# The last 40 steps of an LSTM in a graph layer: one PSUM bank for gate G of each half, another order of products, and moved copies

## The chip, the core and the metric

The kernel runs on one core of a Trainium2 chip. Its engines work side by side, each through its own queue in order: TensorE (PE, with a row PEld for its weight loads), VectorE (DVE), ScalarE (ACT), GpSimd (POOL), and SyncE (SP), which issues DMAs here. The metric is the device time of one execution in microseconds (us); lower is better.

## What is computed

The layer takes 6,250 nodes of 256 features and 100,000 edges. It normalizes the rows, adds a sum over neighbours with a small MLP and a linear attention block, normalizes again, and runs an LSTM over the 6,250 rows as one sequence:

```
def step(carry, xp):                      # xp = x W_ih^T + b_ih + b_hh
    h, c = carry
    gates = xp + h @ W_hh.T
    i, f, g, o = jnp.split(gates, 4, axis=-1)
    c = jax.nn.sigmoid(f) * c + jax.nn.sigmoid(i) * jnp.tanh(g)
    h = jax.nn.sigmoid(o) * jnp.tanh(c)
```

On each output h a two-way argmax of a linear map decides whether h counts; prefix and suffix sums of the counted ones, weighted, are added to 2h and to the input of the LSTM.

## The kernel before

The sequence of 6,250 rows is cut into `NC` = 125 chains of `NS` = 50 rows each, which go through the LSTM together: one step of the kernel handles row s of all chains. Since a chain needs the state that its predecessor ends with, each chain is warmed up by running `WARM` = 40 rows of the predecessor first; a comparison at the end tests whether warmed and true states agree, and a sequential fallback follows if they don't. So there are 90 steps. The first 50 (40 of warm-up, and rows 0 to 9 of the counted pass) compute the inputs' product x W_ih on the way and are not touched here. The warm-up stores that product with the bias to DRAM (`x_d`), and the last 40 steps, rows `KEPT` = 10 to 49, fetch it again (`fetch`, L989, three tiles `x_in` in turn) and add only the product of h with `w_hh`.

In these last 40 steps everything lies with units on the partitions: 256 units are `KD` = 2 halves (a = 0, 1) of 128, and h's 256 units are also the contraction, in two parts (k = 0, 1). A gate g of a half a takes one product for each k, a 128x128 weight block against 128x125 of h; a float32 product shows as two PE records. A step so has 16 products. Gates are I, F, G, O; I, F and O of one half share a PSUM bank, in slots 0 to 2, so that one sigmoid of 375 columns serves the three. G has a bank of its own in which both halves lie, for one tanh of 250 columns. There are two sets of these three banks, one for even and one for odd steps (`sets`, L1083). Two further banks (`pl`) are for the logits.

Before the products of a step can accumulate, its fetched inputs must be in the banks. `into_banks` (L1086) returns three moves: G of both halves, I/F/O of half 0, I/F/O of half 1. In the first two of the 40 steps they are matmuls by an identity with start=True, later they are copies on ACT.

The order on PE, DVE and ACT is as written (a manual schedule). For step s:

- PE (L1109 to L1114): products with k = 0 of G of both halves and of I, F, O of half 0; the same with k = 1; then I, F, O of half 1 with k = 0 and with k = 1; then the two products of the logits of step s - 1. k = 0 reads half 0 of h of the step before, k = 1 reads half 1.
- ACT: tanh of G (L1116); for each half the sigmoid (L1119), one of the moves for step s + 1 (L1121), and the tanh of c (L1127); then the third move (L1132).
- DVE: for each half, `two` (I times tanh G beside F times c, L1124), the add that gives c (L1125), a correction of h of step s - 2 (`weighted`, L882), and h itself (L1130); then `summed` (L884), which thresholds the logits and sums.
- SP: the fetch of step s + 4's inputs at the end of the step, into the tile whose moves the step has just made.

The tile `gc` holds, for each half, tanh of G and c side by side, so that one DVE instruction multiplies both.

Of the kernel before, what the change touches and what calls it, by code (L numbers as in the profile page):

```python
# [14 lines left out]
F32 = mybir.dt.float32  # L15
I32 = mybir.dt.int32
BF16 = mybir.dt.bfloat16
AF = mybir.ActivationFunctionType
# [5 lines left out]
P = 128  # L24
# [3 lines left out]
NC, NS = 125, 50  # L28
HEADS, HC = 8, 32
KD = D // P  # L30
# [51 lines left out]
def gps_layer(ctx: ExitStack, tc: tile.TileContext, x, src, dst, cols, rows, kvln, wqkv, mw1, mw2, gw1, gw2,  # L82
              wih, whh, blstm, out):
    nc = tc.nc
# [7 lines left out]
    ident = big.tile([P, P], F32, name="ident")  # L92
# [66 lines left out]
    with ExitStack() as s1:  # L159
# [54 lines left out]
        with tc.tile_pool(name="ln1", bufs=2) as lp, tc.tile_pool(name="ps0", bufs=6, space=PSUM) as ps:  # L214
# [3 lines left out]
            for i, t in enumerate((src, dst)):  # L218
                s = behind[:, i * (FULL + 1) * P:(i + 1) * (FULL + 1) * P].bitcast(I32).rearrange("p (b e) -> p b e", e=P)
# [35 lines left out]
            for s, to in zip(tiled, (si, drel)):  # L255
                f = late[:, 2 * GE:2 * GE + (FULL + 1) * P].rearrange("p (b e) -> p b e", e=P)
# [126 lines left out]
        ps = s1.enter_context(tc.tile_pool(name="ps1", bufs=4, space=PSUM))  # L383
# [13 lines left out]
        to = [sums[:, k, :N].rearrange("p (c s) -> p s c", s=NS) for k in range(KD)]  # L397
# [5 lines left out]
        def gather(at):  # L403
            g = edge_p.tile([P, D], F32, name="eg", bufs=10)
            nc.gpsimd.indirect_dma_start(out=g, out_offset=None, in_=xn_d[:],  # L405
                                         in_offset=bass.IndirectOffsetOnAxis(ap=at, axis=0))
            return g
# [41 lines left out]
        def kv_job(j):  # L449
# [4 lines left out]
            def product(k, half):  # L454
                at = slice(half * D, (half + 1) * D)
                nc.tensor.matmul(pkv[:r, at], xnT[:, j, k, :], w_qkv[:, k, D:][:, at],  # L456
                                 start=(k == 0 and half == 0), stop=(k == KD - 1), skip_group_check=True)

            yield [partial(product, k, half) for k in range(KD) for half in range(2)], None
            flat = mix_p.tile([P, 2 * D], F32, name="kv", tag="t", bufs=4)  # L460
            nc.vector.tensor_add(flat[:r], pkv[:r], kv_bias[:r])  # L461
# [214 lines left out]
        def bias_job():  # L676

            b_r = [mix_p.tile([P, 2 * D], F32, name="b_r", tag="t", bufs=4) for _ in range(2)]
            for i in range(2):
                nc.sync.dma_start(b_r[i][:2], blstm[:, i * 2 * D:(i + 1) * 2 * D])  # L680
            yield [], None
            yield [], None
            pb = ps.tile([P, BANK], F32, name="mm")

            def product(g):
                at = g * P % (2 * D)
                nc.tensor.matmul(pb[:, g:g + 1], b_r[g * P // (2 * D)][:2, at:at + P], ones[0:2, 0:1], start=(g == 0),
                                 stop=True, skip_group_check=True)

            yield [partial(product, g) for g in range(4 * KD)], None  # L690
            nc.vector.tensor_copy(b_l, pb[:, :4 * KD])
# [41 lines left out]
        with tc.manual_schedule(engines={mybir.EngineType.PE, mybir.EngineType.DVE, mybir.EngineType.Activation}):  # L733
# [3 lines left out]
            while slot < GROUPS - COUNTED or running or before or any(s >= slot for s in starts):  # L737
                g = slot + COUNTED
# [24 lines left out]
        w_hh = big.tile([P, KD, 4 * D], F32, name="w_hh", tag="M2")  # L763
# [5 lines left out]
        with tc.If(held < GROUPS + PAIRS):  # L769
# [15 lines left out]
            with tc.For_i(0, NE, 1) as c:  # L785
# [4 lines left out]
                g = gather(at[:, :1])  # L790
                for n0 in range(0, N + W, W):
# [4 lines left out]
                    for k in range(KD):  # L796
                        nc.tensor.matmul(pm[:, k, :w], g[:, k * P:(k + 1) * P], here[:, 0, :w], start=(k == 0), stop=True,
                                         skip_group_check=True)
# [24 lines left out]
        for a in range(KD):  # L823
            nc.vector.tensor_scalar(scaled[:, a, :], ident, sc[:, a:a + 1], None, op0=ALU.mult)
            nc.tensor.matmul(pb[:, a * P:(a + 1) * P], mean[:, a:a + 1].to_broadcast([P, P]), ident, start=(a == 0),
                             stop=True, skip_group_check=True)
# [12 lines left out]
    I, F, G, O = range(4)  # L839

    SLOT = {I: 0, F: 1, O: 2, G: 3}

    def block(g, a):
        return slice((g * KD + a) * P, (g * KD + a + 1) * P)
# [9 lines left out]
    gc = wl.tile([P, KD, 2, NC], F32, name="gc")  # L854
# [17 lines left out]
    def of_step(s):  # L872
        return hs[:, :, s * NC:(s + 1) * NC]

    def logits(s, pl):
        for k in range(KD):
            nc.tensor.matmul(pl, w_d[:, k, :], of_step(s)[:, k, :], start=(k == 0), stop=(k == KD - 1))

    def weighted(s, i, of, k):

        h_k = of_step(s)[:, k, :]
        nc.vector.scalar_tensor_tensor(h_k, of[:, k, :], half[:, i, k:k + 1], h_k, op0=ALU.mult, op1=ALU.add)  # L882

    def summed(s, pool, pl):  # L884

        w = pool.tile([P, KD, NC], F32, name="w")
        nc.vector.scalar_tensor_tensor(w, pl[:, None, :].to_broadcast([P, KD, NC]), thr, of_step(s), op0=ALU.is_gt,
                                       op1=ALU.mult)
        if s == 0:
            nc.vector.tensor_copy(inc, w)  # L890
        else:
            nc.vector.tensor_add(inc, inc, w)
        for k in range(KD):
            weighted(s, 2, inc, k)
        return w
# [20 lines left out]
    with tc.tile_pool(name="lstm", bufs=2) as rp:  # L916
        AHEAD, FETCH = 3, 3
        s2 = ExitStack()
        ps = s2.enter_context(tc.tile_pool(name="ps3", bufs=4, space=PSUM))
# [69 lines left out]
        def fetch(s):  # L989
            t = rp.tile([P, KD, 4, NC], F32, name="x_in", bufs=FETCH)  # L990
            nc.sync.dma_start(t.rearrange("p k g c -> p (k g c)"), x_d[(s - NS + WARM) * P:(s - NS + WARM + 1) * P, :])
            return t
# [30 lines left out]
        KEPT = NS - WARM  # L1023
# [25 lines left out]
        fetched = []  # L1049
        for i, (s, warm) in enumerate(order):  # L1050
# [18 lines left out]
            if not warm and s > 0:  # L1069
# [7 lines left out]

        s2 = ExitStack()  # L1080
        ps = s2.enter_context(tc.tile_pool(name="ps_k", bufs=1, space=PSUM))
        ps_y = s2.enter_context(tc.tile_pool(name="ps_l", bufs=2, space=PSUM))
        sets = [([ps.tile([P, 3, NC], F32, name=f"pg{i}{a}") for a in range(KD)], ps.tile([P, KD, NC], F32, name=f"pg_g{i}"))  # L1083
                for i in range(2)]

        def into_banks(s, t):  # L1086


            others_a, g_b = sets[s % 2]
            parts = [(g_b, t[:, :, SLOT[G], :])] + [(others_a[a], t[:, a, :SLOT[G], :]) for a in range(KD)]  # L1090
            if s < KEPT + 2:
                return [partial(nc.tensor.matmul, to, ident, of, start=True, stop=False, skip_group_check=True)
                        for to, of in parts]
            return [partial(nc.scalar.copy, to, of) for to, of in parts]

        def product(s, g, a, k):
            others_a, g_b = sets[s % 2]
            to = g_b[:, a, :] if g == G else others_a[a][:, SLOT[g], :]
            nc.tensor.matmul(to, w_hh[:, k, block(g, a)], of_step(s - 1)[:, k, :], start=False, stop=(k == KD - 1),  # L1099
                             skip_group_check=True)  # L1100

        with tc.manual_schedule(engines={mybir.EngineType.PE, mybir.EngineType.DVE, mybir.EngineType.Activation}):
            for bring in into_banks(KEPT, fetched.pop(0)):
                bring()
            fetched.append(fetch(KEPT + FETCH))
            w = None
            for s in range(KEPT, NS):
                more = into_banks(s + 1, fetched.pop(0)) if s + 1 < NS else []
                for k, a_ifo in ((0, 0), (1, 0), (0, 1), (1, 1)):  # L1109
                    gates = [(I, a_ifo), (F, a_ifo), (O, a_ifo)]  # L1110
                    for g, a in gates if a_ifo else [(G, a) for a in range(KD)] + gates:
                        product(s, g, a, k)
                pl = ps_y.tile([P, BANK], F32, name="pl")[:, :NC]
                logits(s - 1, pl)  # L1114
                others_a, g_b = sets[s % 2]
                nc.scalar.activation(gc[:, :, 0, :], g_b, AF.Tanh)  # L1116
                for a in range(KD):
                    gates = rp.tile([P, 4, NC], F32, name="gates")[:, :SLOT[G], :]
                    nc.scalar.activation(gates, others_a[a], AF.Sigmoid)  # L1119
                    for bring in more[a:a + 1]:  # L1120
                        bring()  # L1121

                    two = rp.tile([P, 2, NC], F32, name="two", tag="h_w")
                    nc.vector.tensor_mul(two, gates[:, :2, :], gc[:, a])  # L1124
                    nc.vector.tensor_add(c[:, a, :], two[:, 0, :], two[:, 1, :])  # L1125
                    t_c = rp.tile([P, NC], F32, name="t_c")
                    nc.scalar.activation(t_c, c[:, a, :], AF.Tanh)  # L1127
                    if w is not None:
                        weighted(s - 2, 0, w, a)
                    nc.vector.tensor_mul(of_step(s)[:, a, :], gates[:, SLOT[O], :], t_c)  # L1130
                for bring in more[KD:]:
                    bring()  # L1132
                w = summed(s - 1, rp, pl)
                if s + 1 + FETCH < NS:
                    fetched.append(fetch(s + 1 + FETCH))
            for k in range(KD):
                weighted(NS - 2, 0, w, k)
# [4 lines left out]
        parts = rp.tile([P, 2], F32, name="parts", bufs=1)  # L1142
# [16 lines left out]
    with tc.If(right < 2 * D * (NC - 1)):  # L1159
        one_by_one = ExitStack()  # L1160
        rp = one_by_one.enter_context(tc.tile_pool(name="lstm1", bufs=2))
        ps = one_by_one.enter_context(tc.tile_pool(name="ps3b", bufs=2, space=PSUM))
# [9 lines left out]
        with tc.For_i(0, NC, 1) as c0:  # L1172
# [3 lines left out]
            pg = ps.tile([P, NG, NS], F32, name="pg1")  # L1176
            for g in range(NG):
                at = slice(g * P, (g + 1) * P)
                nc.tensor.matmul(pg[:, g, :], ident, bl_r[:, g, :], start=(g == 0), stop=False, skip_group_check=True)
                for k in range(KD):  # L1180
                    nc.tensor.matmul(pg[:, g, :], w_ih[:, k, at], yb[:, k, :], start=False, stop=False,
                                     skip_group_check=True)
            for t in range(NS):
                for g in range(NG):
                    for k in range(KD):
                        last = h0[:, k:k + 1] if t == 0 else hb[:, k, t - 1:t]
                        nc.tensor.matmul(pg[:, g, t:t + 1], w_hh[:, k, g * P:(g + 1) * P], last, start=False,
                                         stop=(k == KD - 1), skip_group_check=True)
# [96 lines left out]
```

## Time and profile before

| What | us |
|---|---|
| median of 3 runs | 1590.43 (1588.79 to 1592.89) |
| the profiled execution, its own time | 1589.72 |
| span of its profile | 1587.9 |
| last 40 steps, first product to last h | 1337 to 1536 |

The profile is of one execution, and its times add up against its own time. A line of the timeline has the start in us from the span's beginning, the duration, the engine, the line of the kernel, the operation, what it writes and reads, and how many instructions of the same kind were merged; in square brackets stand the idle time in front of it and what ended it. PE records overlap, since matmuls are pipelined and their ends are modelled. A line of waits has who waited for whom, the total in us, how many times, and the longest. A table by stages has the window, its length, and for each engine the busy time with the number of instructions; then the clock granted to TensorE (1.00 is full speed), the share of time in which the DMA engines were busy, and GB/s.

### The profile page before, as it was taken

Reading aid. Unit: us, or ns where it says so; the run is one execution under the profiler, and the core shown is the slowest. Engines: PE = TensorE matmul, PEld = TensorE weight load, DVE = VectorE, ACT = ScalarE, POOL = GpSimd, SP = SyncE. Lnnn points to the kernel's source line nnn. Section 1 sums busy time; section 2 is a strip of 40 time slices with the busy share of each in tenths; the row PEclk is TensorE's granted clock in tenths of the full one; section 3 lists DMA queues with packets and bytes.
Section 4 is the critical chain, followed back from the end, with each engine's and each line's share of the span. In section 5 each row is a group of like instructions: output and inputs, shape, how many; then the busy total and the mean of one; then the engine's idle time right before and its main releaser. Section 6 shows DMA issues by size and latency. Waiting matters only on the chain. (4 is left out here: it accounts for less than half of the span.)

```text
span 1587.9 us, 30599 instructions
## 1 busy us (share of the span) xinstructions
PE 1442.4 (91%) x11164; PEld 1366.3 (86%) x11164; DVE 968.8 (61%) x3002; ACT 600.6 (38%) x1742; POOL 682.0 (43%) x715
## 2 busy tenths in 40 slices
PE   1789999999989999999999689999999999999965
PEld 1488888888989999999989689999999999888864
DVE  6789888888842222222222366666676655777777
ACT  2843334333402222233233234444444433555530
POOL 2177777777777777777777300000000000000005
PEclk9689999999999999999999989999999999999986
DMA  9533333333354555444444321111111100333315
GB/s 249 191 104 103 104 103 104 105 105 105 105 159 137 152 153 149 124 116 123 121 122 117 111 91 53 66 66 53 65 66 63 44 1 27 105 105 105 104 38 163
DMA packets 64644, 165.97 MB, mean 105 GB/s; under 512 B 14350, under 2 KB 29440, under 8 KB 63232
## 3 DMA queue, kind: packets, MB, share of 16 engines
q0 software_dynamic: 31008, 84.71, 18.5%
q1 hardware_dynamic: 29822, 75.08, 14.5%
q10 hardware_dynamic: 3652, 4.10, 1.1%
q8 instruction: 91, 1.49, 0.4%
q14 instruction: 71, 0.58, 0.1%
HBM read 130.56 MB, written 33.28 MB: 103 GB/s over the span
## 5 line engine op out<-in xcount | busy, mean ns | idle before, releaser
L405 POOL DMA_INDIRECT eg<-xn_d,si x646 | 621.4, 962 | 260.6 <-issue 99.3
L426 PE MATMUL pg<-here,eg 128*128 128x96 f32 x2584 | 389.4, 276 | 30.3 <-DMA eg<-xn_d,si 28.1
L426 PEld LDWEIGHTS pg<-here,eg 128*128 128x128 f32 x2584 | 355.7, 194 | 61.0 <-DMA eg<-xn_d,si 29.2
L436 DVE TENSOR_TENSOR sums<-sums,pg 128x192 f32 x162 | 57.4, 354 | 343.9 <-PE pg L426 183.9
L976 PE MATMUL pg<-yT,w_ih 128*128 128x125 f32 x1600 | 189.5, 277 | 0.5 <-ACT yT L967 0.5
L976 PEld LDWEIGHTS pg<-yT,w_ih 128*128 128x128 f32 x1600 | 185.3, 194 | 0.8 <-ACT yT L967 0.8
L942 POOL TENSOR_TENSOR ln_r<-ln_v,minus_half 125x1 f32<-125x1 f32 x50 | 27.3, 550 | 322.9 <-DVE ln_v L936 322.9
L1009 ACT ACTIVATE gates<-pg,b_l 128x125 f32<-128x125 f32 x398 | 111.9, 364 | 132.3 <-PE pg L1000 79.6
L1214 POOL TENSOR_TENSOR xr<-xr,rest_t 125x1024 f32<-125x1024 f32 x8 | 22.9, 2895 | 287.2 <-DVEq L1159 287.2
L1000 PE MATMUL pg<-h_w,w_hh 128*128 128x125 f32 x1248 | 145.9, 275 | 0.1
L1000 PEld LDWEIGHTS pg<-h_w,w_hh 128*128 128x128 f32 x1248 | 143.1, 192 | 0.3 <-DVE x_out L985 0.3
L628 ACT ACTIVATE sums<-mm,vec 128x125 f32<-128x125 f32 x100 | 36.5, 366 | 239.0 <-DVE sums L436 176.4
L1099 PE MATMUL pg<-sums,w_hh 128*128 128x125 f32 x960 | 120.3, 275 | 0.0
L612 PE MATMUL mm<-sums,g 128*128 128x125 f32 x800 | 116.3, 280 | 1.9 <-DVE counts L651 1.1
L1099 PEld LDWEIGHTS pg<-sums,w_hh 128*128 128x128 f32 x960 | 113.6, 192 | 0.0
L623 PE MATMUL mm<-z,g 128*128 128x125 f32 x800 | 112.6, 279 | 0.5 <-ACT z L618 0.5
L612 PEld LDWEIGHTS mm<-sums,g 128*128 128x128 f32 x800 | 103.4, 193 | 5.8 <-issue 1.6
L456 PE MATMUL mm<-m,xr 128*125 128x256 f32 x400 | 107.6, 397 | 0.3 <-DVE counts L651 0.3
L623 PEld LDWEIGHTS mm<-z,g 128*128 128x128 f32 x800 | 99.8, 192 | 0.7 <-ACT z L618 0.7
L464 ACT ACTIVATE mm<-kv 125x512 f32<-125x512 f32 x50 | 30.1, 602 | 183.3 <-DVE kv L461 183.3
L618 ACT ACTIVATE z<-mm,vec 128x125 f32<-128x125 f32 x200 | 56.4, 367 | 94.8 <-PE mm L612 94.8
L416 DVE TENSOR_TENSOR here<-counts,drel 128x384 f32<-128x384 f32 x162 | 90.1, 556 | 0.0
(273 smaller groups left out, 2340.5 us busy)
## 6 DMA issues: line engine op xcount, KB each, us to landing
x_d<-x_out SPq DMA_DIRECT2D x40, 500.0 KB
x_in<-x_d SPq DMA_DIRECT2D x40, 500.0 KB
eg<-xn_d,si POOLq DMA_INDIRECT x646, 2.8
counts<-xn_d SPq DMA_DIRECT2D x16, 384.0 KB
xn<-in_x_dram SPq DMA_DIRECT2D x5, 1120.0 KB
xn_d<-xn SPq DMA_DIRECT2D x5, 1120.0 KB
m<-in_x_dram SPq DMA_DIRECT2D x50, 112.0 KB
out_dram<-o SPq DMA_DIRECT2D x12, 448.0 KB
```

What stands on the lines that cost most here:

```text
L405: nc.gpsimd.indirect_dma_start(out=g, out_offset=None, in_=xn_d[:], in_offset=bass.IndirectOffsetOnAxis(ap=at, axis=0))
L416: nc.vector.tensor_tensor(here[:, :n, :], iota[:, None, :W].to_broadcast([P, n, W]), drel[:, gi * GT:gi * GT + n, None].to_broadcast([P, n ...
L426: nc.tensor.matmul(pg[:, k, :], g[:, k * P:(k + 1) * P], here[:, i, :], start=(i == 0 and k == 0), stop=(i == n - 1), skip_group_check=True)
L436: nc.vector.tensor_add(window, window, pg)
L456: nc.tensor.matmul(pkv[:r, at], xnT[:, j, k, :], w_qkv[:, k, D:][:, at], start=(k == 0 and half == 0), stop=(k == KD - 1), skip_group_chec ...
L612: nc.tensor.matmul(p1[:, m, :], g1[:, k, m * P:(m + 1) * P], sums[:, k, at], start=(m == 0 and k == 0), stop=(k == KD - 1), skip_group_che ...
L618: nc.scalar.activation(z1[:, m, :], p1[:, m, :], AF.Relu, bias=col("gb1", m))
L623: nc.tensor.matmul(p2[:, a, :], g2[:, m, a * P:(a + 1) * P], z1[:, m, :], start=(a == 0 and m == 0), stop=(m == 2 * KD - 1), skip_group_ch ...
L976: nc.tensor.matmul(pg[:, SLOT[g], :], w_ih[:, k, block(g, a)], yT[:, k, s * NC:(s + 1) * NC], start=(i == 0 and k == 0), stop=False, skip_ ...
L1000: nc.tensor.matmul(banks[a][:, SLOT[g], :], w_hh[:, k, block(g, a)], h[:, k, :], start=False, stop=(k == KD - 1), skip_group_check=True)
L1009: nc.scalar.activation(gate[g], pg[:, SLOT[g], :], AF.Tanh if g == G else AF.Sigmoid, bias=bias(g, a))
L1099: nc.tensor.matmul(to, w_hh[:, k, block(g, a)], of_step(s - 1)[:, k, :], start=False, stop=(k == KD - 1), skip_group_check=True)
```

## The change

Four things change in the last 40 steps; the products, activations and DVE work on them stay the same in kind and in amount of data.

- The banks: G of each half has a bank of its own, used by every step (two banks, `bank_g`); I/F/O keep two banks for each half (`bank_o`). It is six banks in all, as before.
- The products: the k = 0 group has G, I, F, O of half 0 and I of half 1; the k = 1 group has G, I, F, O of half 0; then come G of half 1 with both k, F and O of half 1 with k = 0, and I, F, O of half 1 with k = 1.
- The tanh of G is made for each half apart: half 0 before the sigmoid of half 0, half 1 behind it.
- The moves of inputs, now four a step: I/F/O of half 0 of the next step at the head of a step, G of half 0 after the second tanh of G, G of half 1 and I/F/O of half 1 behind the sigmoid of half 1, ahead of the tanh of c of half 1. I/F/O are moved by PE in the first two steps, G in the first step only.

```diff
-        sets = [([ps.tile([P, 3, NC], F32, name=f"pg{i}{a}") for a in range(KD)], ps.tile([P, KD, NC], F32, name=f"pg_g{i}"))
-                for i in range(2)]
...
+        bank_g = [ps.tile([P, NC], F32, name=f"pg_g{a}") for a in range(KD)]
+        bank_o = [[ps.tile([P, SLOT[G], NC], F32, name=f"pg{i}{a}") for a in range(KD)] for i in range(2)]
+
+        def bring(s, t, gate_g, a):
+
+            to, of = (bank_g[a], t[:, a, SLOT[G], :]) if gate_g else (bank_o[s % 2][a], t[:, a, :SLOT[G], :])
+            if s < KEPT + (1 if gate_g else 2):
+                nc.tensor.matmul(to, ident, of, start=True, stop=False, skip_group_check=True)
+            else:
+                nc.scalar.copy(to, of)
+
+        def products(s, *of):
+            for g, a, k in of:
+                to = bank_g[a] if g == G else bank_o[s % 2][a][:, SLOT[g], :]
+                nc.tensor.matmul(to, w_hh[:, k, block(g, a)], of_step(s - 1)[:, k, :], start=False, stop=(k == KD - 1),
+                                 skip_group_check=True)
...
             for s in range(KEPT, NS):
-                more = into_banks(s + 1, fetched.pop(0)) if s + 1 < NS else []
-                for k, a_ifo in ((0, 0), (1, 0), (0, 1), (1, 1)):
-                    gates = [(I, a_ifo), (F, a_ifo), (O, a_ifo)]
-                    for g, a in gates if a_ifo else [(G, a) for a in range(KD)] + gates:
-                        product(s, g, a, k)
+                more = s + 1 < NS
+                t = fetched.pop(0) if more else None
+                if more:
+                    bring(s + 1, t, False, 0)
+                products(s, (G, 0, 0), (I, 0, 0), (F, 0, 0), (O, 0, 0), (I, 1, 0))
+                products(s, (G, 0, 1), (I, 0, 1), (F, 0, 1), (O, 0, 1))
+                products(s, (G, 1, 0), (G, 1, 1), (F, 1, 0), (O, 1, 0), (I, 1, 1), (F, 1, 1), (O, 1, 1))
                 pl = ps_y.tile([P, BANK], F32, name="pl")[:, :NC]
                 logits(s - 1, pl)
-                others_a, g_b = sets[s % 2]
-                nc.scalar.activation(gc[:, :, 0, :], g_b, AF.Tanh)
                 for a in range(KD):
+                    if a == 0:
+                        nc.scalar.activation(gc[:, 0, 0, :], bank_g[0], AF.Tanh)
                     gates = rp.tile([P, 4, NC], F32, name="gates")[:, :SLOT[G], :]
-                    nc.scalar.activation(gates, others_a[a], AF.Sigmoid)
-                    for bring in more[a:a + 1]:
-                        bring()
+                    nc.scalar.activation(gates, bank_o[s % 2][a], AF.Sigmoid)
+                    if a == 0:
+                        nc.scalar.activation(gc[:, 1, 0, :], bank_g[1], AF.Tanh)
+                    if more:
+                        bring(s + 1, t, True, a)
+                    if a and more:
+                        bring(s + 1, t, False, 1)
...
-                for bring in more[KD:]:
-                    bring()
                 w = summed(s - 1, rp, pl)
```

More of the change, by code (lines that the diff above doesn't have):

```diff
@@ L1082, in gps_layer @@
         ps_y = s2.enter_context(tc.tile_pool(name="ps_l", bufs=2, space=PSUM))
-        sets = [([ps.tile([P, 3, NC], F32, name=f"pg{i}{a}") for a in range(KD)], ps.tile([P, KD, NC], F32, name=f"pg_g{i}"))
-                for i in range(2)]
-        def into_banks(s, t):
-            others_a, g_b = sets[s % 2]
[L1090 to L1100, printed above, removed]
+        bank_g = [ps.tile([P, NC], F32, name=f"pg_g{a}") for a in range(KD)]
[11 more added lines that the diff above has]
+                                 skip_group_check=True)
         with tc.manual_schedule(engines={mybir.EngineType.PE, mybir.EngineType.DVE, mybir.EngineType.Activation}):
-            for bring in into_banks(KEPT, fetched.pop(0)):
-                bring()
+            t = fetched.pop(0)
+            for gate_g in (False, True):
+                for a in range(KD):
+                    bring(KEPT, t, gate_g, a)
             fetched.append(fetch(KEPT + FETCH))
@@ L1107, in gps_layer @@
             for s in range(KEPT, NS):
-                more = into_banks(s + 1, fetched.pop(0)) if s + 1 < NS else []
-                for k, a_ifo in ((0, 0), (1, 0), (0, 1), (1, 1)):
-                    gates = [(I, a_ifo), (F, a_ifo), (O, a_ifo)]
-                    for g, a in gates if a_ifo else [(G, a) for a in range(KD)] + gates:
-                        product(s, g, a, k)
+                more = s + 1 < NS
[5 more added lines that the diff above has]
+                products(s, (G, 1, 0), (G, 1, 1), (F, 1, 0), (O, 1, 0), (I, 1, 1), (F, 1, 1), (O, 1, 1))
                 pl = ps_y.tile([P, BANK], F32, name="pl")[:, :NC]
                 logits(s - 1, pl)
-                others_a, g_b = sets[s % 2]
-                nc.scalar.activation(gc[:, :, 0, :], g_b, AF.Tanh)
                 for a in range(KD):
+                    if a == 0:
+                        nc.scalar.activation(gc[:, 0, 0, :], bank_g[0], AF.Tanh)
                     gates = rp.tile([P, 4, NC], F32, name="gates")[:, :SLOT[G], :]
-                    nc.scalar.activation(gates, others_a[a], AF.Sigmoid)
-                    for bring in more[a:a + 1]:
-                        bring()
+                    nc.scalar.activation(gates, bank_o[s % 2][a], AF.Sigmoid)
[5 more added lines that the diff above has]
+                        bring(s + 1, t, False, 1)
                     two = rp.tile([P, 2, NC], F32, name="two", tag="h_w")
@@ L1130, in gps_layer @@
                     nc.vector.tensor_mul(of_step(s)[:, a, :], gates[:, SLOT[O], :], t_c)
-                for bring in more[KD:]:
-                    bring()
                 w = summed(s - 1, rp, pl)
```

## The prediction

> **What bounds the kernel now.** The page comes first. TensorE is busy 91% of the span, which says little about one stage, so the second view is the table by stages. The changed code runs from 1337 to 1536 us, and the table is asked for its steady part.
>
> ```profile
> span 1587.9 us, 30599 instructions
> ...
> 1345.00:1530.00 185.00, 170.10 (x1350) 156.06 (x1349) 146.69 (x448) 107.23 (x301) 0.00 (x0) 1.00 0.33 99
> ```
>
> In 185 us the order is PE, weight load, DVE, ACT, POOL. None is full: a step takes 4.945 us (the tanh of gate G starts at 1349.68 in one step and at 1532.63 thirty-seven steps later), and the clock is granted in full. So the stage is a loop of waits, and the third view, the list of waits in the same stretch, says where an engine runs dry.
>
> ```profile
> ACT t_c L1127 <- DVE gc L1125: 36.8, 75, 0.6
> ...
> ACT gates L1119 <- PE pg L1099: 10.7, 37, 0.3
> ```
>
> L1119, the sigmoid, runs twice a step (74 times in 37 steps) but waits for TensorE only 37 times: the second half never does. The fourth view, the timeline of one step, shows why. Columns are start, duration, engine, line, operation, out<-in, count.
>
> ```profile
> 1386.48 0.47 ACT L1119 ACTIVATE gates<-pg 128x375 f32<-128x375 f32 x1
> ...
> 1386.84 0.47 ACT L1121 COPY pg<-x_in 128x375 f32<-128x375 f32 x1
> ...
> 1386.95 0.71 PE L1099 MATMUL pg_g<-sums,w_hh 128*128 128x125 f32 x4 [0.29 <-DVE sums L1130]
> 1386.97 0.42 DVE L1124 TENSOR_TENSOR two<-gates,gc 128x250 f32<-128x250 f32 x1
> ...
> 1387.43 0.29 DVE L1125 TENSOR_TENSOR gc<-two 128x125 f32<-128x125 f32 x1
> 1387.50 0.83 PE L1099 MATMUL pg<-sums,w_hh 128*128 128x125 f32 x6
> ...
> 1387.75 0.31 ACT L1127 ACTIVATE t_c<-gc 128x125 f32<-128x125 f32 x1 [0.44 <-DVE gc L1125]
> 1387.97 0.47 ACT L1132 COPY pg<-x_in 128x375 f32<-128x375 f32 x1
> 1388.10 0.29 DVE L1130 TENSOR_TENSOR sums<-gates,t_c 128x125 f32<-128x125 f32 x1
> ...
> 1388.44 0.71 PE L1099 MATMUL pg_g<-sums,w_hh 128*128 128x125 f32 x4
> ...
> 1388.99 2.17 PE L1099 MATMUL pg<-sums,w_hh 128*128 128x125 f32 x18
> 1389.25 0.38 ACT L1116 ACTIVATE gc<-pg_g 128x250 f32<-128x250 f32 x1 [0.81 <-PE pg_g L1099]
> ...
> 1389.92 0.48 ACT L1119 ACTIVATE gates<-pg 128x375 f32<-128x375 f32 x1 [0.29 <-PE pg L1099]
> 1390.30 0.37 ACT L1121 COPY pg_g<-x_in 128x250 f32<-128x250 f32 x1
> 1390.43 0.42 DVE L1124 TENSOR_TENSOR two<-gates,gc 128x250 f32<-128x250 f32 x1 [0.56 <-ACT gates L1119]
> ...
> 1390.89 0.29 DVE L1125 TENSOR_TENSOR gc<-two 128x125 f32<-128x125 f32 x1
> ...
> 1391.21 0.31 ACT L1127 ACTIVATE t_c<-gc 128x125 f32<-128x125 f32 x1 [0.54 <-DVE gc L1125]
> 1391.42 0.47 ACT L1119 ACTIVATE gates<-pg 128x375 f32<-128x375 f32 x1
> ```
>
> One product is two PE records. Half 1 of h ends at 1388.39 (1388.10 + 0.29); call that zero of the step. Then 10 records (G of both halves, I/F/O of half 0, all k=1) lead to sigmoid 0 at +1.53; two, add and tanh of c follow at +2.04, +2.50, +2.82; sigmoid 1 starts +3.03, 0.21 behind that tanh, its queue neighbour. From sigmoid 1 to the end of the next half 1 is 1.91 (1386.48 to 1388.39), so 3.03 + 1.91 = 4.94, the period.
>
> How long could sigmoid 1 wait for PE instead? The 18 records last 2.17 and one lasts 0.275, so they are (2.17 - 0.275)/17 = 0.1115 apart. ACT starts 0.10 after a record's end (G: 1388.44 + 0.71 to 1389.25; sixth record: 1389.82 to 1389.92). The 18th ends at 1391.16, so sigmoid 1 could start at 1391.26, +2.87. It starts at +3.03: **0.16 us of slack**, and this number decides the case.
>
> **The change, part by part.** (1) Order of products. Before, 10 records stand between h's half 1 and sigmoid 0; after, 8 (G, I, F, O of half 0). Two records of 0.1115 go: sigmoid 0, two, add and tanh of c0 come 0.22 earlier (+1.30, +1.81, +2.27, +2.60). ACT is then free for sigmoid 1 at +2.81. But the full run from h's half 1 to the last product stays 22 records (8 + 14 against 10 + 12): G and I of half 1 only trade places across the k groups. So sigmoid 1 is next held by PE at +2.87, and the gain is 0.16, not 0.22. Its tail of 1.91 is unchanged: period 4.78. The k=0 group stays 10 records; it starts with h's half 0 (+3.23 now) and ends its issue near +4.49, before the new half 1 at +4.78.
>
> (2) The tanh of G in two. No 128x125 tanh from PSUM without a bias is in the trace; the forms of 250 and 375 columns take 0.38 and 0.48, so 0.29 by a line through them; the nearest row with a bias takes 0.36 (L1009). I take 0.29. The first lies at +0.63 (2 records), in ACT's idle 0.81. The second is queued behind sigmoid 0 and waits for record 12: starts about +1.75. Behind it on ACT are the G copy and tanh of c0. ACT is free by about +2.15, tanh of c0 is due at +2.60: a cover of 0.45, so I cost it at zero. Without the cover every 0.1 would be 0.1 on tanh of c0, of which 0.06 would still hide behind PE.
>
> (3) Copies. One G copy of 0.37 becomes two; by 0.37 and 0.475 for 250 and 375 columns, 0.27 each. I/F/O of half 0 (0.47) moves from behind sigmoid 1 to the head of the step, in ACT's idle time after the last tanh of c. Behind sigmoid 1 now stand the G copy of half 1 and I/F/O of half 1, the latter moved in front of tanh of c1. Sigmoid 1 plus both, with no overlap at all, is 0.475 + 0.27 + 0.47 = 1.22; with the 0.1 overlaps that neighbours show it is near 0.95. Tanh of c1 is due 1.27 after sigmoid 1 (1386.48 to 1387.75). So zero, in both ends. PE's new early product of half 1 (I, k=0) needs that last copy at about +4.27; the copy ends near +3.90. Were it late, all PE work behind it, G of k=1 included, would be late; it may be 0.6 late before the new half 1 (+4.78) is kept waiting.
>
> (4) The single G bank. Refilling it waits for the tanh just in front on the same engine: no cross-engine wait. G of half 0 is refilled by +2.3 and needed by PE at +3.28; half 1's by +3.5 and needed in the next step.
>
> (5) SP's fetch of inputs waits for the last copy, which now ends about 1.1 earlier in the step; the fetch issues earlier. The first copy of a fetched tile is wanted earlier too, but some 10 us remain from issue, against about 3 (issue at 1388.46; the step before, DMA was busy from about 1384.3 to 1386.3 after an issue at 1383.5). POOL is idle here. Zero.
>
> (6) The first step. One PE copy (2 x 0.31) goes in front of its products and three (about 1.8) behind them become one. Before, those held up the next products (h's half 0 ready at 1341.45, products at 1342.80). Followed by the same rows, the next step's half 1 ends some 0.4 earlier than 1348.83, net of the late start. Ends: 0 and 0.8.
>
> **A rule against it.** The trace shows ACT 0.10 after both PE groups it waits for, and records 0.1115 apart across a group's end, so an additional announced group costs nothing. The Trainium skill, "TensorE: Matmul & The Clock Gate", "The cost: per-tile semaphore tail", says increments at the ends of matmuls serialize, about 26 ns each. The new order has one more announced group ahead of sigmoid 1. By the row the step gains 0.16, by the rule 0.13; 38 steps give 6.1 or 5.1. I follow the row: the page speaks of many tiles ending at once, which no row here shows.
>
> **The sum.** 38 intervals between ends of half 1 x 0.16 = 6.1, plus 0.4 = 6.5. The profiled execution took 1589.72 (span 1587.9 and 1.8 around it), so 1583.2; the median shown is 0.7 above it, so **1583.9**. Bounds: starts of an engine after a semaphore vary by up to 0.06 in this trace (tanh of c comes 0.09 after add in the first steps, 0.03 later), so a step gains 0.10 to 0.22: 3.8 to 9.2 in all, 1581 to 1587. A measurement of this kernel can tell about 0.3%, 4.8 us, from no change.
>
> **Rivals.** *Forecast, 0.70*: PE becomes the bound of sigmoid 1.
> *The gain is eaten at once, 0.18.* If dependences on tile gc are kept for the whole tile, two of half 0 waits for the second tanh of G, which ends at +2.04: two at +2.07 instead of +2.04 before, and each step loses 0.03: +1.1 - 0.4, about 1591. Against it speaks an earlier stage, where parts of one tile are separate: the product of I and G starts before the last two of four gates are done.
>
> ```profile
> 1279.16 1.13 ACT L1009 ACTIVATE gates<-pg,b_l 128x125 f32<-128x125 f32 x4 [3.85 <-PE pg L1000]
> ...
> 1279.82 0.29 DVE L1015 TENSOR_TENSOR gates<-gates 128x125 f32<-128x125 f32 x1 [0.53 <-ACT gates L1009]
> ```
>
> *Slower, 0.12: ACT's queue behind sigmoid 1.* Two copies now stand in front of tanh of c1. They have 0.32 to spare, and 0.16 is gained, so they decide from 0.48 of extra time a step. Were each copy to cost 0.36 more than its row (by colliding with matmuls that write PSUM), the step would lose 0.24: 9 us, 1599. No row shows such stretching: copies at 1386.84 and 1390.30 take 0.47 and 0.37 with PE writing beside them.
> That the change does nothing is excluded by the two records that leave the path.
>
> **How the numbers follow.** Of the forecast's 0.70, 0.64 lies beyond 4.8 us and 0.06 within; the second case gives 0.15 within and 0.02 slower, 0.01 faster; the third gives 0.10 slower and 0.02 within: faster 0.65, same 0.23, slower 0.12. The range takes the forecast's 1581 to 1587 and reaches over half of the second case, to 1590.5.
>
> **What would show it.** A period of 4.78; tanh of G twice a step; sigmoid 0 0.22 earlier after h's half 1; sigmoid 1 waiting for PE in nearly every step, by about 0.06; the gap from sigmoid 1 to tanh of c1 still 1.27; PE's wait for half 1 of h grown from 0.30 to about 0.36. I am wrong if two of half 0 waits past sigmoid 0, if the gap of 1.27 grows, if sigmoid 1 starts later than +2.9, or if the early I product waits for its copy.

## The result, and the profile after

The change makes the kernel faster: 1584.37 us against 1589.55 in the median of nine runs each, a ratio of 0.9962 with a 95% interval of 0.9945 to 0.9979, all of it below 1. The medians differ by 5.2 us; the ratio makes it some 6. The forecast, 1583.9, is 0.5 us off. The profiled execution of the changed kernel shows where it went.

The page first: its span, against the 1587.9 of before.

```profile
span 1581.2 us, 30563 instructions
```

The span is 6.7 shorter. The stage itself gained more. From its first PE move of inputs (1335.32 before, 1336.36 after) to the sum on agreement behind it (`agree`, 1541.1 and 1533.7) it takes 205.8 and 197.3: 8.4 less. In two more profiles of the changed kernel (under E3) it takes 197.3 and 197.4. In this execution 1.0 was lost ahead of the stage and 0.7 behind it, in code that the change does not touch.

The timeline of one step after the change (columns as before):

```profile
1382.09 0.29 DVE L1137 TENSOR_TENSOR sums<-gates,t_c 128x125 f32<-128x125 f32 x1
...
1382.44 0.49 PE L1098 MATMUL pg_g<-sums,w_hh 128*128 128x125 f32 x2 [0.18 <-DVE sums L1137]
...
1382.76 0.83 PE L1098 MATMUL pg<-sums,w_hh 128*128 128x125 f32 x6
...
1382.96 0.28 ACT L1120 ACTIVATE gc<-pg_g 128x125 f32<-128x125 f32 x1 [0.53 <-PE pg_g L1098]
...
1383.43 0.61 PE L1098 MATMUL pg_g<-sums,w_hh 128*128 128x125 f32 x4
1383.63 0.48 ACT L1122 ACTIVATE gates<-pg 128x375 f32<-128x375 f32 x1 [0.39 <-PE pg L1098]
...
1383.88 1.28 PE L1098 MATMUL pg<-sums,w_hh 128*128 128x125 f32 x10
1384.08 0.28 ACT L1124 ACTIVATE gc<-pg_g 128x125 f32<-128x125 f32 x1
1384.15 0.42 DVE L1131 TENSOR_TENSOR two<-gates,gc 128x250 f32<-128x250 f32 x1 [0.28 <-ACT gates L1122]
1384.25 0.27 ACT L1093 COPY pg_g<-x_in 128x125 f32<-128x125 f32 x1
...
1384.92 0.31 ACT L1134 ACTIVATE t_c<-gc 128x125 f32<-128x125 f32 x1 [0.41 <-DVE gc L1132]
...
1385.19 0.48 ACT L1122 ACTIVATE gates<-pg 128x375 f32<-128x375 f32 x1
...
1385.58 0.27 ACT L1093 COPY pg_g<-x_in 128x125 f32<-128x125 f32 x1
...
1385.77 0.47 ACT L1093 COPY pg<-x_in 128x375 f32<-128x375 f32 x1
...
1385.93 1.06 PE L1098 MATMUL pg<-sums,w_hh 128*128 128x125 f32 x8
...
1386.49 0.31 ACT L1134 ACTIVATE t_c<-gc 128x125 f32<-128x125 f32 x1 [0.25 <-DVE gc L1132]
```

Take 1382.38, the end of half 1 of h (1382.09 + 0.29), as zero of the step. Sigmoid 0 starts at +1.25 (it was +1.53), the tanh of c0 at +2.54 (+2.82), sigmoid 1 at +2.81 (+3.03), the tanh of c1 1.30 behind it (it was 1.27). The next step's half 1 ends at 1387.12, so the period here is 4.74. Over 31 steps, from the tanh of G at 1378.2 to the one at 1525.1, it is 4.74 as well, against 4.944 of before (30 steps, 1384.30 to 1532.63). The 38 intervals behind the second step, at 0.205 each, make 7.8. The first two steps gave 0.6 more: from the first PE move to the end of half 1 of the second step it took 13.51 before and 12.87 after. Together that is 8.4, all that the stage gained.

### The profile page after: what moved, and what is told of

It is laid out like the page before. It is cut to its first block, busy times and chain, and to the rows that moved or that the text cites. A ratio compares the mean times of both kernels' runs of the same rounds, so it can differ in the third digit from the quotient of the medians.

```text
span 1581.2 us, 30563 instructions
## 1 busy us (share of the span) xinstructions
PE 1443.4 (91%) x11164; PEld 1366.0 (86%) x11164; DVE 968.4 (61%) x3002; ACT 612.4 (39%) x1822; POOL 682.6 (43%) x715
## 5 line engine op out<-in xcount | busy, mean ns | idle before, releaser
L1098 PE MATMUL pg<-sums,w_hh 128*128 128x125 f32 x960 | 126.8, 275 | 0.0
L1098 PEld LDWEIGHTS pg<-sums,w_hh 128*128 128x128 f32 x960 | 116.8, 192 | 0.0
```

## The experiments

The experiments ran in three sets, each with the kernel before beside it on the same chip (E1, E2 and E3; E4 and E5; E3 repeated). In the first two sets the gathers ahead of the LSTM end about 160 us later for every kernel, before included, so their times stand near 1750; why is not known. Each ratio is against the kernel before of the same set, and the step is read from the profile. The clock granted to TensorE in the steady part of the last 40 steps is 1.00 in every profile.

**E1, the old order in the new banks.** The products go back to the order of before; banks, moves and the split tanh stay as changed.

```diff
-                products(s, (G, 0, 0), (I, 0, 0), (F, 0, 0), (O, 0, 0), (I, 1, 0))
-                products(s, (G, 0, 1), (I, 0, 1), (F, 0, 1), (O, 0, 1))
-                products(s, (G, 1, 0), (G, 1, 1), (F, 1, 0), (O, 1, 0), (I, 1, 1), (F, 1, 1), (O, 1, 1))
+                products(s, (G, 0, 0), (G, 1, 0), (I, 0, 0), (F, 0, 0), (O, 0, 0))
+                products(s, (G, 0, 1), (G, 1, 1), (I, 0, 1), (F, 0, 1), (O, 0, 1))
+                products(s, (I, 1, 0), (F, 1, 0), (O, 1, 0), (I, 1, 1), (F, 1, 1), (O, 1, 1))
```

> The new banks, moves and split tanh, with the products in the order of before: 10 records again between half 1 of h and sigmoid 0. Theory (two terms: 0.16 us a step from the two records taken off the path, the rest from ACT starting 0.03 to 0.04 after PE instead of 0.10, because the activations have one wait instead of two): only the second term is left. Sigmoid 0 at +1.47, sigmoid 1 right behind the tanh of c0 at +2.97 with no PE wait, period 4.89, some 2.1 us less than before. Rival A (the order is all of the gain): period 4.94, no difference from before. Rival B (the banks or the copies bring it, not the order): period 4.73, as after.

Measured: ratio 0.9985 (0.9976 to 0.9994), some 2.6 us less than before; period 4.883 (30 steps, 1547.2 to 1693.7). In its timeline sigmoid 0 stands 0.04 behind the sixth record of the x18 row (1640.00 + 5 x 0.1115 + 0.275 = 1640.83), and sigmoid 1 is again 0.21 behind the tanh of c0:

```profile
1640.00 2.17 PE L1098 MATMUL pg<-sums,w_hh 128*128 128x125 f32 x18
1640.87 0.48 ACT L1122 ACTIVATE gates<-pg 128x375 f32<-128x375 f32 x1 [0.62 <-PE pg L1098]
...
1642.16 0.31 ACT L1134 ACTIVATE t_c<-gc 128x125 f32<-128x125 f32 x1 [0.47 <-DVE gc L1132]
1642.37 0.46 ACT L1122 ACTIVATE gates<-pg 128x375 f32<-128x375 f32 x1
```

So the order is worth 4.883 - 4.74 = 0.14 a step, and the rest of the change 0.06. Both rivals fall: the period is neither 4.94 nor 4.73.

**E2, the kernel before with its activations waiting once.** The 0.06 was not in the prediction. A semaphore is the sign by which one instruction tells others that it is done. In the records of the trace before, 118 of the 120 tanhs of G and sigmoids wait for two semaphores, PE's and one that ACT itself sets (presumably for the copy that filled the bank); after, 158 of 160 wait for one, PE's. The view of the sigmoid's line shows the second wait as a row of its own, on ACT's sequencer (before, then after):

```profile
L1119 ACTq EVENT_SEMAPHORE  x66: 17/17/17, 1360.2 to 1519.8; - x66
```

```profile
L1122 ACT ACTIVATE gates<-pg x68: 483/483/485, 1360.0 to 1517.8; 128x375 f32<-128x375 f32 x68
```

Before has one such semaphore instruction for each of its 66 sigmoids in that stretch; after, the 68 sigmoids have no such row. E2 takes them away in the kernel before, by nothing but one tiny copy at the end of the step:

```diff
                 for bring in more[KD:]:
                     bring()
+                if KEPT + 2 <= s + 1 < NS:
+                    own = rp.tile([P, 1], F32, name="own")
+                    nc.scalar.copy(own, sets[(s + 1) % 2][0][1][:, 0, 0:1])
```

> The kernel before, with one more ACT copy of 128x1 at the end of each step that reads what the last copy wrote; its wait on ACT itself takes that wait off the tanh of G and the sigmoids, which then wait for PE alone. Theory of the two waits: the rows of event semaphores in front of L1116 and L1119 go, both start 0.03 to 0.04 after PE's end, the period falls from 4.945 to 4.89, some 2.1 us. Rival (the 0.06 comes from the banks or from how PE's ends are modelled): the period stays 4.945, or grows if the extra instruction costs something.

Measured: ratio 0.9988 (0.9976 to 0.9999); period 4.883 (30 steps, 1549.5 to 1696.0). The semaphore rows are gone from all steps but the first two, which the edit leaves as they were, and the tanh of G stands 0.04 behind its last record (1641.54 + 0.71 = 1642.25), where it was 0.10:

```profile
1641.54 0.71 PE L1099 MATMUL pg_g<-sums,w_hh 128*128 128x125 f32 x4
```

```profile
1642.29 0.38 ACT L1116 ACTIVATE gc<-pg_g 128x250 f32<-128x250 f32 x1 [0.56 <-PE pg_g L1099]
```

With the old banks, the old order and the old copies the step is as short as E1's. So the lost wait accounts for all that the banks, the split tanh and the moved copies brought by themselves; no other net gain or cost of theirs shows. How they take the wait off, no run shows by itself. A reading that fits: all 78 copies into the G banks wait for ACT's own semaphore in the trace after, as they do in E1 and as the tiny copy does here, and what ACT has waited for once, its later instructions need not wait for again.

**E3, one more product early.** F of half 1, k = 0, moves from the last group to the first:

```diff
-                products(s, (G, 0, 0), (I, 0, 0), (F, 0, 0), (O, 0, 0), (I, 1, 0))
+                products(s, (G, 0, 0), (I, 0, 0), (F, 0, 0), (O, 0, 0), (I, 1, 0), (F, 1, 0))
...
-                products(s, (G, 1, 0), (G, 1, 1), (F, 1, 0), (O, 1, 0), (I, 1, 1), (F, 1, 1), (O, 1, 1))
+                products(s, (G, 1, 0), (G, 1, 1), (O, 1, 0), (I, 1, 1), (F, 1, 1), (O, 1, 1))
```

> After, with F of half 1, k = 0, moved into the first group too: 20 records instead of 22 between half 1 of h and the last product. Theory (sigmoid 1 is held by PE, by 0.06): sigmoid 1 starts 0.21 behind the tanh of c0 instead of 0.27, period 4.67, 2.3 us less than after; the first group of 12 records still ends its issue 0.06 before half 1 of h. Rival (the gap of 0.27 belongs to ACT): period 4.73 as after, or longer if the first group now holds up half 1's products.

> The changed kernel once more, beside the others: period 4.73, about 1584.

Measured: the period is 4.66 (32 steps, 1534.2 to 1683.4), and 4.74 for the changed kernel beside it (31 steps, 1538.6 to 1685.4). Sigmoid 1 follows the tanh of c0 by 0.22 (0.27 in the changed kernel), as in E1, where it stands right behind that tanh:

```profile
1629.41 0.31 ACT L1134 ACTIVATE t_c<-gc 128x125 f32<-128x125 f32 x1 [0.41 <-DVE gc L1132]
1629.63 0.46 ACT L1122 ACTIVATE gates<-pg 128x375 f32<-128x375 f32 x1
```

So PE did hold sigmoid 1 after the change, by some 0.06; with two records fewer it is held by ACT again. The stage, from the first PE move to `agree`, takes 194.5 against 197.3. The times of this set did not tell the two apart: 1745.95 and 1745.27, ratios 0.9960 (0.9945 to 0.9976) and 0.9957 (0.9942 to 0.9972). The repetition:

> The order with F of half 1, k = 0, in the first group, once more. Its step was 0.07 shorter than the changed kernel's in the profile (4.66 against 4.74), and its stage 3 us, but the two times could not be told apart. Theory: 3 us less than the changed kernel, some 10.5 less than before. Rival (the time in the stage comes back behind it): the same time as the changed kernel.

> The changed kernel beside it, on the same chip: period 4.74, some 7 us less than before.

Measured: 1579.74 (1579.15 to 1580.99 in 6 runs), ratio 0.9920 (0.9904 to 0.9936), and for the changed kernel 1584.29 (1583.11 to 1587.18), ratio 0.9948 (0.9931 to 0.9964). Here the ranges of the two lie apart, by 4.5 us in the median, against 3 expected; against the kernel before, the medians are 13.1 and 8.6 lower, where 10.5 and 7 were expected. The stage is again 194.5 against 197.4. The shorter step and stage are thus shown by both sets; that the whole time is shorter than the changed kernel's is shown by one set of two.

**E4, the copy of half 1 put back.** The copy of I, F, O of half 1 goes behind the tanh of c of half 1, where it was before; its product stays early.

```diff
-                    if a and more:
-                        bring(s + 1, t, False, 1)
...
+                if more:
+                    bring(s + 1, t, False, 1)
                 w = summed(s - 1, rp, pl)
```

> After, with the copy of I, F, O of half 1 put back behind the tanh of c of half 1, as before; its early product I of half 1, k = 0, stays. Theory: that copy ends at about +4.79 of the step, the early product cannot start before +4.83, and PE in order holds up the products with k = 1 behind it by 0.36: period 5.09, slower than before by some 5.7 us. Rival (the place of the copy is a matter of taste, its cover is elsewhere): 4.73, as after.

Measured: ratio 1.0011 (1.0002 to 1.0021), some 2 us slower than before where 5.7 were expected; period 5.01 (30 steps, 1546.3 to 1696.6). A new wait appears on PE, on ACT's copy, in the first group:

```profile
1645.00 0.31 ACT L1132 ACTIVATE t_c<-gc 128x125 f32<-128x125 f32 x1 [0.64 <-DVE gc L1130]
1645.21 0.87 ACT L1093 COPY pg<-x_in 128x375 f32<-128x375 f32 x2
1645.34 0.29 DVE L1135 TENSOR_TENSOR sums<-gates,t_c 128x125 f32<-128x125 f32 x1
1645.73 0.49 PE L1098 MATMUL pg<-sums,w_hh 128*128 128x125 f32 x2 [0.45 <-ACT pg L1093]
1646.06 0.39 PE L1098 MATMUL pg_g<-sums,w_hh 128*128 128x125 f32 x2
```

Half 1 of h ends at 1645.63, and the products that need it stand at 1646.06 behind the early product that waits for its copy. Against the changed kernel the step loses 0.27, not 0.36: after a wait, PE's second record starts 0.21 behind the first (0.49 for two records, less 0.275 for one) instead of 0.11, and here the early product takes that upon itself before the products with k = 1. The moved copy is a condition of the new order, not a gain of its own.

**E5, a copy more behind sigmoid 1.**

```diff
                     if a and more:
                         bring(s + 1, t, False, 1)
+                        fill = rp.tile([P, 2, NC], F32, name="fill", bufs=1)
+                        nc.scalar.copy(fill, t[:, 1, :2, :])
```

> After, with one more ACT copy (128x250 to SBUF, used by nobody) between the last copy and the tanh of c of half 1. Theory: ACT has 0.36 to spare there and the copy takes 0.28 of it: period 4.73, as after. Rival (ACT's queue behind sigmoid 1 has no room, and the moved copy is paid for): 0.28 a step, period 5.01, some 10 us more.

Measured: ratio 0.9963 (0.9949 to 0.9977), period 4.74 (31 steps, 1541.3 to 1688.2). The extra copy fits without moving the tanh of c1, which starts 1.30 behind sigmoid 1 as without it, 0.04 behind the add on DVE that it waits for. It just fits: the tanh starts 0.08 before the extra copy's end, about the overlap of the other neighbours on ACT (0.06 to 0.11 in these timelines).

```profile
1633.55 0.48 ACT L1122 ACTIVATE gates<-pg 128x375 f32<-128x375 f32 x1
...
1634.12 0.47 ACT L1093 COPY pg<-x_in 128x375 f32<-128x375 f32 x1
...
1634.52 0.29 DVE L1134 TENSOR_TENSOR gc<-two 128x125 f32<-128x125 f32 x1
1634.53 0.40 ACT L1130 COPY fill<-x_in 128x250 f32<-128x250 f32 x1
...
1634.85 0.31 ACT L1136 ACTIVATE t_c<-gc 128x125 f32<-128x125 f32 x1
```

## Why the prediction was right

*The path.* Two records leave the way to sigmoid 0, and sigmoid 1 turns from ACT-bound to PE-bound. This is what happened: E1 shows that 0.14 of the gain goes with the order, E3 that PE is the new bound. No view lists the wait of sigmoid 1 as such, since ACT's tanh, 1384.92 to 1385.23, is still counted busy when the sigmoid starts at 1385.19. It is seen in two distances: from the tanh to the sigmoid, 0.27 against 0.21, and from PE's last record (1383.88 + 1.28 = 1385.16) to the sigmoid, 0.03, as at sigmoid 0.

*The size.* The sum had 0.16 a step, the stage gave 0.205. The mis-sized term is ACT's start 0.10 behind PE, which part 1 took over unchanged from the rows of before. It is 0.03 to 0.04 after (1383.59 to 1383.63 at sigmoid 0), because the second wait went. So sigmoid 1 came at +2.81 instead of the predicted +2.87. From there to the end of half 1 it took 1.93, not 1.91. The 0.02 is sigmoid 1 itself: started by PE it lasts 0.48, right behind another ACT instruction 0.46 to 0.47, as before and in E3. 0.16 + 0.06 - 0.02 makes the 0.20, and E1 and E2 measure the same split: 0.14 for the order, 0.06 for the wait. The stage total was 8.4 against 6.5. That the forecast time was met within 0.5 us is luck. The medians here differ by 5.2, not 6.5, and the median of before came 0.9 lower than the one that the forecast started from. In the other two sets with the changed kernel the medians differ by 8.5 and 8.6, near the stage's 8.4, and the nine runs of before alone spread over 8.9.

*The missing 0.06 stood in the prediction.* Its bounds name tanhs of c that start 0.09 behind their add in the first steps and 0.03 later, and count this as scatter. It is not: before, three of the 80 tanhs of c have a second wait, and these three start 0.09 behind, the other 77 all 0.03.

```profile
L1127 ACTq EVENT_SEMAPHORE  x3: 17/17/17, 1342.3 to 1348.1; - x3
```

*The rule against it.* From the first record that waits for half 1 to the last product, PE takes 2.445 before (1388.44 to 1390.885) and 2.445 after (1382.44 to 1384.885, the latter 1383.88 + 1.28 - 0.275), with four groups in it that ACT waits for instead of three. ACT's start behind PE is also the same after (0.03 to 0.04) as in E1, which has one group less. The 26 ns of the Trainium skill, "TensorE: Matmul & The Clock Gate", "The cost: per-tile semaphore tail", do not appear here, as far as modelled ends can tell; many tiles that end at once are not in this kernel.

*Costed at nothing.* The two tanhs of G last 0.28, the short copies 0.27 (0.29 and 0.27 were taken), and tanh of c0 still waits 0.41 for DVE behind them. Behind sigmoid 1 there is room for one copy more than the change put there (E5). The early product of half 1 finds its copy made: the copy ends at 1386.24, and the product, the last two of the x8 records, starts at about 1386.60 (1385.93 + 6 x 0.1115). That this cover is real, and what it costs when gone, is E4. No idle time of ACT in the steady part is put down to the fetch of inputs.

*The first steps* gave 0.64 where 0.4 was set. With the old order (E1) they give 0.35, so that term was sized well; the other 0.29 comes with the new order, which these two steps have as well and which the sum gave to the 38 intervals behind them only.

*The rivals.* That two of half 0 would wait for the second tanh of G: it starts at 1384.15, while that tanh runs from 1384.08 to 1384.36, so it does not. That ACT's queue behind sigmoid 1 would be the loss: E5 excludes it.

*The signs.* Tanh of G runs twice a step. The period is 4.74 (4.78 named), sigmoid 0 comes 0.28 earlier (0.22 named, and 0.06 for the wait). PE's weight load waits 0.37 for half 1 of h, where 0.36 was named (before, then after):

```profile
1388.44 0.52 PEld L1099 LDWEIGHTS pg_g<-sums,w_hh 128*128 128x128 f32 x4 [0.30 <-DVE sums L1130]
```

```profile
1382.44 0.30 PEld L1098 LDWEIGHTS pg_g<-sums,w_hh 128*128 128x128 f32 x2 [0.37 <-DVE sums L1137]
```

One sign of being wrong came true to the letter: the gap from sigmoid 1 to the tanh of c1 grew, from 1.27 to 1.30. It was meant for ACT's queue; the growth comes from the longer sigmoid, and in E3, with the same copies in the queue, the gap is 1.27 again.

## What to carry to other kernels

In a loop of waits, compute for each wait how far the second-latest releaser is behind the latest: the order took 0.22 from one path, of which 0.14 was gained (0.16 in the sum), because the other path was 0.16 away. Moving work earlier in the queue of an engine paid here only because what it reads was moved earlier as well (E4). And look for semaphore instructions on an engine's sequencer in front of an instruction that ends a critical wait: a second wait there, even on something long done, was part of the path here.

## What was not expected of the hardware

A tanh of G or sigmoid that PE releases starts, with two waits, 0.10 behind PE's modelled end, and with a single one 0.03 to 0.04, in all ten traces. It is not a matter of the kernel or the line: after, the one tanh of G of half 0 with two waits starts 0.10 behind, the other 39 start 0.04 behind. For the tanh of c, which waits for DVE, it is 0.09 and 0.03. Before, the second wait cost the step 0.06 (E2). One dependent 128x1 copy in idle time (0.16) took the wait off three activations a step.
